# A graph-attention and expert layer on one core: edge loop in written order, node stage in 69 steps

## The chip, the cores and the metric

One NeuronCore of a Trainium2 chip runs the whole program. The metric is the device time of one execution in microseconds (us). The kernel before takes 4170.29 us, the median of 14 runs (4151.29 to 4191.23).

Engines are named as in the profile: PE is the matrix engine (PEld its weight loads), DVE the vector engine, ACT the activation engine, POOL the engine that also writes the descriptors of indirect DMAs, SP the engine that issues most other DMAs. Each engine takes its instructions in one fixed order and waits at the head of its queue.

## The reference, cut to what matters

There are 6250 nodes of 256 features and 206250 edges, sorted by destination. The layer is a transformer convolution over the edges (8 heads of 32), a feed-forward block (FFN) with a gelu, and a mixture of a shared MLP and the best two of four experts.

```python
x0 = layernorm(x)
q, xr, k, v = x0 @ Wq.T + bq, x0 @ Wskip.T + bskip, x0 @ Wk.T + bk, x0 @ Wv.T + bv
e = edge_attr @ We.T                                # 206250 x 256, in heads 8 x 32
alpha = sum(q[dst] * (k[src] + e), axis=-1) / sqrt(32)
w = softmax(alpha over the edges of each dst)
out = segment_sum((v[src] + e) * w, dst)
beta = sigmoid([out, xr, out - xr] @ Wbeta.T)
y = ln1(x0 + beta * xr + (1 - beta) * out)
h = x + ln2(y + gelu(y @ W1.T + b1) @ W2.T + b2)    # gelu by erf, 1024 inner columns
z = layernorm(h)
gates = softmax(z @ gW + gb); top two, softmaxed again
return h + shared_mlp(z) + sum(top two experts(z) * weight)
```

## The kernel before

A first stage (lines 100 to 304) builds tables from the edge list and projects the nodes; it writes `kv_d` (k and v of each node, 2 KB a row), `q_d` and `rn_d` to DRAM. Then `sorted_edges` runs. It has two parts in one Python loop.

**The edge loop.** The edges are 403 blocks of 512, four tiles of 128 each. One pass of the loop works on several blocks at once, as a pipeline over passes:

- `load(i)`, L689 and L691: POOL gathers the k and v rows of block i into the buffer `X` with four indirect DMAs of 128 rows, SP loads the edge features beside them. Pool `fx` has five buffers, and block i+4 is loaded in pass i, so the load of a block waits until `gather` of the block five before it has read its buffer.
- `group(g)`, L645 to L683: for each four blocks, the q rows they need (`qq`, L648) are gathered, stored and loaded again in another layout (`qs`, `qw`), the indicator `oh` (L671) and the folded weights `ws` (L678, L681) are made. The function is a generator; the loop takes one step of it in a pass.
- `score(i+1)`: PE spreads q over the edges (`qg`, L705), DVE multiplies with k (`prod`, L711) and sums over each head (L713).
- `turn(i)`: four PE transposes (L721), an ACT copy to `xT` (L723). `rows(i)`: PE makes the scores (L733), DVE takes their maximum (L737). `weigh(i)`: ACT exponentials with a row sum (L744). `turn_back(i)`: two PE transposes (L752), an ACT copy to `pT` (L754). `gather(i)`: eight PE products (L767, sixteen records in the trace) add up v and edge features by destination. `keep(i)`: DVE picks each head's columns (L775, L778), ACT copies the rest (L777), SP stores the partial sums to `part_d` (L779).

**The node stage.** When all edges of two 125-node blocks are done (`follow`), a generator `ffn` for that pair joins the list `nodes`; there are 25 pairs. `advance(1)`, called three times in a pass, runs the first generator of the list to its next `yield`. Its first part is `merge`: four indirect DMAs (L788) fetch the partial sums of a block into `A`, which has one buffer; DVE weights and adds them (L795 to L821); PE and ACT apply the edge weights (L825 to L833). Then come the gate beta (L405 to L420), the first layer norm (L390 to L429), the FFN (L436 to L463), the second and third norm, the gates, and the shared and expert layers (L484 to L576).

In the FFN one step holds all eight inner column groups: for each, two PE products (L448, four records) and one ACT gelu of 128x250 (L450). After them ACT loads the table set of exponentials again (L451). All PSUM results of the node stage and of `group` share one pool, `f_g`, of three banks.

The order in which the code issues instructions is not the order in which the engines get them: a scheduler orders the whole loop by its own priorities and its own estimate of times, and only what `keep_in_program_order` names stays in place.

Of the kernel before, what the change touches and what calls it, by code (L numbers as in the profile page):

```python
# [40 lines left out]
def gnn_moe_layer(ctx: ExitStack, tc: tile.TileContext, a: dict, out: bass.AP):  # L41
# [322 lines left out]
    def ffn(b0, p3, bank, attention):  # L364
# [67 lines left out]
        def transposed(v, name):  # L432
            tp = bank([128, 2, M])
            for j in range(n):
                for k in range(2):
                    nc.tensor.transpose(tp[:, k, j * NB : (j + 1) * NB],  # L436
                                        v[:, j, k * 128 : (k + 1) * 128], ident[:NB, :NB])
            vT = p3.tile([128, 2, M], F32, name=name, tag="yT")
            nc.scalar.copy(vT, tp)
            return vT  # L440

        yT = transposed(y, "yT")
        yield
        h1 = p3.tile([128, FF // 128, M], F32, name="h1", tag="h1")
        for f in range(FF // 128):
            ps = bank([128, M])
            for k in range(2):
                nc.tensor.matmul(ps, w1[:, k, f * 128 : (f + 1) * 128], yT[:, k, :],  # L448
                                 start=(k == 0), stop=(k == 1))
            nc.scalar.activation(h1[:, f, :], ps, AF.Gelu, bias=b1c[:, f : f + 1])  # L450
        tc.keep_in_program_order(nc.scalar.preload_act_table_set("natural_log_exp_and_others"))  # L451
# [4 lines left out]
        for j in range(n):  # L456
            ps = bank([NB, D])
            for f in range(FF // 128):
                nc.tensor.matmul(ps, h1[:, f, j * NB : (j + 1) * NB], w2[:, f, :],  # L459
                                 start=(f == 0), stop=(f == FF // 128 - 1))  # L460
                if f == FF // 256 - 1:
                    yield
            nc.vector.tensor_tensor(y2[:, j, :], ps, y[:, j, :], ALU.add)  # L463
            yield
# [12 lines left out]
        zT = transposed(z, "zT")  # L477
# [3 lines left out]
        lg = bank([NB, n, NE])  # L481
        for j in range(n):
            for k in range(2):
                nc.tensor.matmul(lg[:, j, :], zT[:, k, j * NB : (j + 1) * NB], gw[:, k, :],  # L484
                                 start=(k == 0), stop=(k == 1))

# [26 lines left out]
        yield  # L513
# [9 lines left out]
        yield  # L523
# [12 lines left out]
        yield  # L536
# [17 lines left out]
        yield  # L554
        wp = bank([128, NE // 2, M])
        for j in range(n):
            for g in range(NE // 2):
                nc.tensor.transpose(wp[:, g, j * NB : (j + 1) * NB], wx[:, j, 2 * g : 2 * g + 2].rearrange("p e d -> p (e d)"),
                                    ident[:NB, :NB])
        nc.vector.tensor_tensor(e2, e2, wp, ALU.mult)  # L560
        wt = bank([NE + 1, M])
        for j in range(n):
            nc.tensor.transpose(wt[:, j * NB : (j + 1) * NB], w[:, j, :], ident[:NB, :NB])
        wT = p3.tile([NE + 1, M], F32, name="wT", tag="wT")
        nc.scalar.copy(wT, wt)
        yield
        for j in range(n):
            cs = slice(j * NB, (j + 1) * NB)
            ps = bank([NB, D])
            nc.tensor.matmul(ps, s2[:, cs], s3w, start=True, stop=False)  # L570
            for g in range(NE // 2):
                nc.tensor.matmul(ps, e2[:, g, cs], e3w[:, g, :], start=False, stop=False)  # L572
            nc.tensor.matmul(ps, wT[:, cs], e3b, start=False, stop=True)  # L573
            nc.vector.tensor_tensor(x2[:, j, :], ps, x2[:, j, :], ALU.add)
        yield
        nc.sync.dma_start(rows_of(out), x2)  # L576

    def sorted_edges(ctx):
# [50 lines left out]
        with tc.tile_pool(name="fd", bufs=3, space=bass.MemoryType.DRAM) as fd, tc.tile_pool(name="fg", bufs=2) as fg, \  # L629
                tc.tile_pool(name="fg1", bufs=1) as fg1, \  # L630
                tc.tile_pool(name="fx", bufs=5) as fx, tc.tile_pool(name="fw", bufs=2) as fw, \
# [5 lines left out]
                tc.tile_pool(name="f_g", bufs=3, space=PSUM) as f_g:  # L637
            groups = {}
            state = {}

            def bank(shape):
                return f_g.tile(shape, F32, name="gp", tag="gp")

            def group(g):
# [4 lines left out]
                                             in_offset=bass.IndirectOffsetOnAxis(ap=idq[:, g : g + 1], axis=0))  # L649
                yield  # L650
# [14 lines left out]
                yield  # L665
                qw = fg.tile([64, GQ * 2, D], BF16, name="qw")
                for u in range(T // 2):
                    nc.sync.dma_start(qw[32 * u : 32 * u + 3 * W],
                                      qs[64 * u : 64 * (u + 1)].rearrange("(m j) (s d) -> (j s) m d", j=W, s=3))
                oh = fg.tile([64, GQ * 2, 128], BF16, name="oh")  # L670
                nc.vector.tensor_scalar(oh[:, : 2 * n], rb[:, : 2 * n], j3[:64], None, op0=ALU.is_equal)  # L671
                yield
# [22 lines left out]
            def score(i):  # L695
# [4 lines left out]
                prod = fw.tile([128, T, D], F32, name="prod")  # L700
# [15 lines left out]
            def turn(i):  # L716
# [5 lines left out]
                xT = fw.tile([K, T, 128], F32, name="xT")  # L722
# [17 lines left out]
            def weigh(i):  # L740
                X3, os, sp = state[i]
                P = fw.tile([128, T // 2, 128], F32, name="P")
# [28 lines left out]
            def keep(i):  # L771

                os, op = state.pop(i)
                ov = fw.tile([128, T // 2, 4, C], F32, name="ov")
                nc.vector.tensor_tensor(ov, op[:, :, : 4 * C].rearrange("p u (h c) -> p u h c", c=C),  # L775
                                        hmc.rearrange("p (o h) c -> p o h c", o=1).to_broadcast([128, T // 2, 4, C]), ALU.mult)
                nc.scalar.copy(os[:, :, C : C + ED], op[:, :, 4 * C :])  # L777
                nc.vector.tensor_reduce(os[:, :, 0:C], ov.rearrange("p u h c -> p u c h"), AX.X, ALU.add)  # L778
# [3 lines left out]
            def merge(b0, n, at):  # L782

                for j in range(n):
                    A = fm.tile([NB, 2, H * PR], F32, name="A", tag="A")
                    for s in range(2):
                        for i in range(2):
                            nc.gpsimd.indirect_dma_start(  # L788
                                out=A[:, s, i * (H // 2 * PR) : (i + 1) * (H // 2 * PR)], out_offset=None,
                                in_=part_d[: 2 * W * tiles_to(b0 + j)], in_offset=bass.IndirectOffsetOnAxis(ap=idp[:NB, b0 + j, s, i : i + 1], axis=0))  # L790
                        yield
                    for _ in range(4):
                        yield
# [18 lines left out]
                    ov = fm.tile([NB, 2, H, C], F32, name="ov", tag="ov2")  # L812
                    oa = fm.tile([NB, 2, H, ED], F32, name="oa", tag="oa")
                    for s in range(2):
                        for v, c0, m in ((ov, 0, C), (oa, C, ED)):
                            nc.vector.tensor_tensor(v[:, s], A4[:, s, :, c0 : c0 + m],  # L816
                                                    w[:, s].rearrange("p (h o) -> p h o", o=1)
                                                    .to_broadcast([NB, H, m]), ALU.mult)
                        yield
                    nc.vector.tensor_tensor(oa[:, 0], oa[:, 0], oa[:, 1], ALU.add)  # L820
                    nc.vector.tensor_tensor(ov[:, 0], ov[:, 0], ov[:, 1], ALU.add)  # L821
                    yield
                    tp = bank([128, H // 2, NB])
                    for i in range(H // 2):
                        nc.tensor.transpose(tp[:, i, :], oa[:, 0, 2 * i : 2 * i + 2].rearrange("p h d -> p (h d)"),  # L825
                                            ident[:NB, :NB])
                    oT = fm.tile([128, H // 2, NB], F32, name="oT", tag="oT")
                    nc.scalar.copy(oT, tp)
                    yield
                    ps = bank([NB, D])  # L830
                    for i in range(H // 2):
                        nc.tensor.matmul(ps[:, i * 2 * C : (i + 1) * 2 * C], oT[:, i, :], web[:, i, :], start=True, stop=True)  # L832
                    nc.vector.tensor_tensor(at[:, j].rearrange("p (h c) -> p h c", c=C), ps.rearrange("p (h c) -> p h c", c=C),  # L833
                                            ov[:, 0], ALU.add)
# [5 lines left out]
            def follow(i):  # L840

                for b0 in range(0, NBLK, 2):
                    b = min(b0 + 1, NBLK - 1)
                    if (tiles_to(b) - 1) // T == i:
                        nodes.append(ffn(b0, p3, bank, merge))
# [7 lines left out]


            AHEAD = 4
            prep = []
            for i in range(-1 - GQ, B + 2):
                if i % GQ == GQ - 2 and 0 <= (i + GQ + 2) // GQ < NG or i == -1 - GQ:
                    prep.append(group(0 if i < -GQ else (i + GQ + 2) // GQ))
                if 0 <= i - 2 < B:  # L860
                    keep(i - 2)
                    follow(i - 2)
                if 0 <= i - 1 < B:
                    weigh(i - 1)
                if 0 <= i + 1 < B:
                    score(i + 1)
                if 0 <= i < B:
                    turn(i)
                if 0 <= i - 1 < B:
                    turn_back(i - 1)  # L870
                advance(1)
# [3 lines left out]
                if 0 <= i - 1 < B:  # L875
                    gather(i - 1)
                if 0 <= i + AHEAD < B:
                    load(i + AHEAD)
                for g in prep[:1]:
                    if next(g, prep) is prep:  # L880
                        prep.pop(0)
# [3 lines left out]
    def any_edges(ctx):  # L885
# [207 lines left out]
        with tc.tile_pool(name="p3", bufs=2) as p3, tc.tile_pool(name="p3_ps", bufs=3, space=PSUM) as p3_ps:  # L1093
            def bank(shape):
                return p3_ps.tile(shape, F32, name="gp", tag="gp")

            for b0 in range(0, NBLK, 2):
                for _ in ffn(b0, p3, bank, fetch):
# [62 lines left out]
```

## Time and profile before

| what | us |
|---|---|
| median of 14 runs | 4170.29 |
| the profiled execution | 4151.98 |
| its span, first to last instruction | 4150.1 |
| before the first L767 | 593.8 |
| from the first to the last L767, 403 passes | 3422.4 |
| after the last L767 | 133.9 |

The three last rows are cut at the starts of the first and the last L767 record. The loop takes 3422.4 / 403 = 8.49 us a pass, or 3422.4 / 25 = 136.9 us for each pair of node blocks. Busy times of the whole span: PE 3039.2 us (73%), DVE 2408.0 (58%), POOL 1979.0 (48%), ACT 1448.7 (35%). The busy time of PE is a model of pipelined instructions, so it says little by itself.

A group row of the profile reads: line, engine, operation, tile written <- tiles read, shapes, count, then busy time and the mean of one in ns, then the idle time just before and what ended it. A row of a windows view has, after the stretch and its length, the busy time of PE, PEld, DVE, ACT and POOL with the number of instructions in brackets, the granted clock of PE as a share, the share of time the 16 DMA engines were busy, and GB/s.

### The profile page before, as it was taken

What the parts mean: (1) busy time and instruction counts of PE and PEld (TensorE: products, weight loads), DVE (VectorE), ACT (ScalarE), POOL (GpSimd) and SP (SyncE); (2) the same over time, 40 slices, a digit from 0 to 9 for tenths busy, and PEclk for the clock granted to TensorE, in tenths of its full rate; (3) what the DMA queues carried; (4) which work ended last, traced back from release to release, by engine and by line L of the source; (5) the groups of instructions that cost most, each with busy time, mean ns of one, the idle gap of its engine ahead of it and who ended that gap; (6) DMA issues with size and microseconds to landing.
All of it is one profiled execution on the core that took longest, in us unless ns stands there. A gap on an engine that the chain in (4) does not pass through costs nothing. (4 is left out here: it accounts for less than half of the span.)

```text
span 4150.1 us, 59098 instructions
## 1 busy us (share of the span) xinstructions
PE 3039.2 (73%) x19362; PEld 1916.7 (46%) x19363; DVE 2408.0 (58%) x5624; ACT 1448.7 (35%) x4313; POOL 1979.0 (48%) x2030
## 2 busy tenths in 40 slices
PE   2566637777778778777877787788778777877876
PEld 1222224454455445544554554455445454544555
DVE  9223235666556656666666566656556665666663
ACT  0111113344333334333433343334334433443332
POOL 0111136654645565555555555555555555555530
PEclk9877856576677677667777776677667767766777
DMA  0333368866766676767767776766676677667730
GB/s 20 113 113 124 123 195 237 217 188 183 205 174 173 189 211 185 195 188 206 192 189 202 201 191 187 203 185 178 179 200 187 181 202 207 181 190 209 200 98 10
DMA packets 611830, 727.33 MB, mean 175 GB/s; under 512 B 384196, under 2 KB 461309, under 8 KB 611514
## 3 DMA queue, kind: packets, MB, share of 16 engines
q0 software_dynamic: 169040, 495.21, 42.6%
q1 hardware_dynamic: 425153, 196.53, 17.9%
q10 hardware_dynamic: 17321, 31.70, 2.1%
q8 instruction: 158, 2.59, 0.3%
q14 instruction: 158, 1.29, 0.1%
HBM read 614.28 MB, written 108.73 MB: 174 GB/s over the span
## 5 line engine op out<-in xcount | busy, mean ns | idle before, releaser
L689 POOL DMA_INDIRECT X<-kv_d,srcT x1612 | 1562.0, 969 | 1257.5 <-issue 380.3
L711 DVE TENSOR_TENSOR prod<-qg,X 128x512 f32<-128x512 f32 x806 | 539.6, 681 | 62.2 <-PE qg L705 38.1
L767 PE MATMUL o<-X,pT 128*32 128x192 f32 x6448 | 502.6, 442 | 17.5 <-ACT pT L754 13.8
L713 DVE TENSOR_REDUCE X<-prod 128x32 f32<-128x1024 f32 x403 | 486.6, 1207 | 0.5
L733 PE MATMUL m<-xT,ws 80*64 80x128 f32 x3224 | 372.8, 367 | 141.4 <-issue 107.9
L705 PE MATMUL qg<-qw,oh 24*128 24x256 bf16 x1612 | 300.3, 341 | 229.1 <-DVE prod L711 132.1
L744 ACT ACTIVATE P<-m,os 128x128 f32<-128x128 f32 x806 | 289.0, 363 | 427.1 <-issue 335.8
L721 PE MATMUL m<-ident,X 128*80 128x128 f32 x1612 | 359.1, 362 | 84.9 <-issue 58.6
L723 ACT COPY xT<-m 80x512 f32<-80x512 f32 x403 | 234.2, 581 | 478.1 <-PE m L721 185.8
L733 PEld LDWEIGHTS m<-xT,ws 80*64 80x64 f32 x3224 | 237.0, 180 | 352.3 <-issue 259.1
L775 DVE TENSOR_TENSOR ov<-o,hmc 128x256 f32<-128x256 f32 x403 | 169.2, 420 | 393.0 <-PE m L752 159.9
L788 POOL DMA_INDIRECT A<-part_d,idp x200 | 249.2, 1246 | 211.8 <-DVE oa L816 89.6
L752 PE MATMUL m<-ident,P 128*128 128x128 f32 x806 | 227.4, 366 | 153.3 <-ACT P L744 76.0
L721 PEld LDWEIGHTS m<-ident,X 128*80 128x80 f32 x1612 | 213.0, 154 | 210.6 <-issue 144.3
L767 PEld LDWEIGHTS o<-X,pT 128*32 128x32 f32 x6448 | 210.3, 136 | 196.3 <-issue 98.6
L737 DVE TENSOR_REDUCE os<-m 128x2 f32<-128x256 f32 x403 | 168.5, 418 | 228.0 <-issue 137.2
L448 PE MATMUL gp<-yT,w 128*128 128x250 f32 x800 | 233.6, 452 | 24.6 <-ACT h L450 12.0
L705 PEld LDWEIGHTS <-oh 24*128 24x128 bf16 x1612 | 77.7, 98 | 351.9 <-issue 341.3
L752 PEld LDWEIGHTS m<-ident,P 128*128 128x128 f32 x806 | 132.0, 184 | 227.9 <-ACT P L744 120.7
L778 DVE TENSOR_REDUCE os<-ov 128x64 f32<-128x256 f32 x403 | 236.0, 586 | 0.1
L448 PEld LDWEIGHTS gp<-yT,w 128*128 128x128 f32 x800 | 179.7, 233 | 68.2 <-issue 16.4
L299 POOL TENSOR_TENSOR qr<-qt 125x256 f32<-125x256 f32 x50 | 33.4, 669 | 359.9 <-ACT qt L297 340.9
(235 smaller groups left out, 4661.0 us busy)
## 6 DMA issues: line engine op xcount, KB each, us to landing
X<-in_edge_dram SPq DMA_DIRECT2D x403, 128.0 KB
part_d<-os SPq DMA_DIRECT2D x403, 98.0 KB
X<-kv_d,srcT POOLq DMA_INDIRECT x1612
qs<-qq SPq DMA_DIRECT2D x101, 192.0 KB
qw<-qs SPq DMA_DIRECT2D x202, 96.0 KB
q_d<-qt ACTq DMA_DIRECT2D x50, 312.5 KB
rb<-rel_d SPq DMA_DIRECT2D x200, 64.0 KB
rn_d<-rn SPq DMA_DIRECT2D x50, 250.0 KB
```

Of the source, the lines that this page charges most:

```text
L448: nc.tensor.matmul(ps, w1[:, k, f * 128 : (f + 1) * 128], yT[:, k, :], start=(k == 0), stop=(k == 1))
L689: nc.gpsimd.indirect_dma_start(out=X3[:, t, : 2 * D], out_offset=None, in_=kv_d, in_offset=bass.IndirectOffsetOnAxis(ap=srcT[:, i, t : t + ...
L705: nc.tensor.matmul(qgs[u][:, c, :], oh[rows, 2 * q + c, :], qw[rows, 2 * q + c, :], start=True, stop=True)
L711: nc.vector.tensor_tensor(prod[:, 2 * u : 2 * u + 2, :].rearrange("p t (s c) -> p t s c", s=2), qgs[u].rearrange("p t (s c) -> p t s c", s ...
L713: nc.vector.tensor_reduce(X3[:, :, 2 * D + ED : 2 * D + ED + H], prod.rearrange("p t (h c) -> p t h c", c=C), AX.X, ALU.add)
L721: nc.tensor.transpose(xp[:K, t, :], X3[:, t, 2 * D :], ident)
L733: nc.tensor.matmul(sp[(t % 2) * 64 : (t % 2 + 1) * 64, t // 2, :], ws[:, t // 2 * 2 * GQ + 2 * q + t % 2].rearrange("k g w h -> k (g w h)" ...
L744: nc.scalar.activation(P[:, u, :], sp[:, u, :], AF.Exp, bias=os[:, u, PR - 1 : PR], accum_out=os[:, u, PR - 2 : PR - 1])
L752: nc.tensor.transpose(pp[:, u, :], P[:, u, :], ident)
L767: nc.tensor.matmul(op[32 * r : 32 * (r + 1), u, :].rearrange("p (s c) -> p s c", s=3), pT[:, u, 32 * r : 32 * (r + 1)], va, start=True, st ...
L778: nc.vector.tensor_reduce(os[:, :, 0:C], ov.rearrange("p u h c -> p u c h"), AX.X, ALU.add)
L788: nc.gpsimd.indirect_dma_start(out=A[:, s, i * (H // 2 * PR) : (i + 1) * (H // 2 * PR)], out_offset=None, in_=part_d[: 2 * W * tiles_to(b0 ...
```

## The change

- The whole edge loop stands in `tc.manual_schedule()`: every engine gets its instructions in the order in which the code issues them.
- The node stage is cut into more steps, 69 for a pair, and `advance(1)` is called five times in a pass. The eight inner column groups are eight steps; each ends with ACT adding the bias (`Identity`) instead of the gelu. One gelu over all 2000 columns follows, then the table load.
- PSUM: `f_g` has two banks, and a new pool `f_h` of one bank (`held`) takes the results that live over several steps. Most of these now have a `yield` between the PE work and the instruction that reads it.
- `fetch` is a stage of its own: A has two buffers, one for each block of a pair, and is fetched four passes after the pair's last block, two indirect DMAs in each of four passes. `ffn` starts ten passes after it. `merge` multiplies in place in `A`.
- `fx` has six buffers and block i+5 is loaded in pass i. `prod`, `xT`, `P` and `ov` have one buffer instead of two.
- `weigh(i)` moves from the start of pass i+1 to the end of pass i. `keep` is split; its ACT copy and store are in `store`, after `turn_back`. `group` starts one pass earlier and has empty steps between its DMAs and their use.

```diff
-            nc.scalar.activation(h1[:, f, :], ps, AF.Gelu, bias=b1c[:, f : f + 1])
-        tc.keep_in_program_order(nc.scalar.preload_act_table_set("natural_log_exp_and_others"))
+            nc.scalar.activation(h1[:, f, :], ps, AF.Identity, bias=b1c[:, f : f + 1])
+            yield
+        nc.scalar.activation(h1, h1, AF.Gelu)
+        ins = nc.scalar.preload_act_table_set("natural_log_exp_and_others")
+        if pin:
+            tc.keep_in_program_order(ins)
...
-            ps = bank([NB, D])
+            ps = held([NB, D])
             for f in range(FF // 128):
                 nc.tensor.matmul(ps, h1[:, f, j * NB : (j + 1) * NB], w2[:, f, :],
                                  start=(f == 0), stop=(f == FF // 128 - 1))
-                if f == FF // 256 - 1:
+                if f % 2 == 1:
                     yield
...
-                tc.tile_pool(name="fx", bufs=5) as fx, tc.tile_pool(name="fw", bufs=2) as fw, \
+                tc.tile_pool(name="fx", bufs=6) as fx, tc.tile_pool(name="fw", bufs=2) as fw, \
...
-                tc.tile_pool(name="f_g", bufs=3, space=PSUM) as f_g:
+                tc.tile_pool(name="f_g", bufs=2, space=PSUM) as f_g, \
+                tc.tile_pool(name="f_h", bufs=1, space=PSUM) as f_h, tc.manual_schedule():
+            AHEAD = 5
...
-            def merge(b0, n, at):
-
-                for j in range(n):
-                    A = fm.tile([NB, 2, H * PR], F32, name="A", tag="A")
+            def fetch(b0):
+
+                rows_of[b0] = []
+                for b in range(b0, min(b0 + 2, NBLK)):
+                    A = fm.tile([NB, 2, H * PR], F32, name="A", tag=f"A{b - b0}")
+                    rows_of[b0].append(A)
                     for s in range(2):
                         for i in range(2):
                             nc.gpsimd.indirect_dma_start(
...
                         yield
...
-                        for v, c0, m in ((ov, 0, C), (oa, C, ED)):
-                            nc.vector.tensor_tensor(v[:, s], A4[:, s, :, c0 : c0 + m],
-                                                    w[:, s].rearrange("p (h o) -> p h o", o=1)
-                                                    .to_broadcast([NB, H, m]), ALU.mult)
+                        nc.vector.tensor_tensor(A4[:, s, :, : C + ED], A4[:, s, :, : C + ED],
+                                                w[:, s].rearrange("p (h o) -> p h o", o=1)
+                                                .to_broadcast([NB, H, C + ED]), ALU.mult)
                         yield
```

The new loop, whole:

```python
prep = []
fetched = []
for i in range(-1 - 2 * GQ, B + 10):
    g, r = divmod(i + 2 * GQ - 1, GQ)
    if r == 0 and 0 < g < NG or i == -1 - 2 * GQ:
        prep.append(group(max(g, 0)))
    if 0 <= i - 2 < B:
        keep(i - 2)
    if 0 <= i + 1 < B:
        score(i + 1)
    advance(1)
    each(prep)
    if 0 <= i < B:
        turn(i)
    if 0 <= i - 1 < B:
        turn_back(i - 1)
    if 0 <= i - 2 < B:
        store(i - 2)
    advance(1)
    if 0 <= i < B:
        rows(i)
    advance(1)
    if 0 <= i - 1 < B:
        gather(i - 1)
    if 0 <= i < B:
        weigh(i)
    advance(1)
    if 0 <= i + AHEAD < B:
        load(i + AHEAD)
    fetched += [fetch(b0) for b0 in after(i - 4)]
    each(fetched)
    nodes += [ffn(b0, p3, bank, held, merge, pin=False) for b0 in after(i - 10)]
    advance(1)
advance(1000)
```

`each` takes one step of every generator in its list; `after(i)` names the pairs whose last edge block is i.

## The prediction

> **What bounds the kernel now.** I read the page first, then the loop cut into stretches, then POOL's waits, then the timeline of one slow pass.
>
> ```profile
> core 0: us, PE busy (x) PEld busy (x) DVE busy (x) ACT busy (x) POOL busy (x), PEclk, DMA share, GB/s
> 593.80:4016.20 3422.40, 2667.42 (x18382) 1719.25 (x18380) 2126.05 (x4857) 1336.06 (x4026) 1875.24 (x1882) 0.71 0.70 192
> 1694.40:1700.40 6.00, 4.83 (x39) 2.38 (x37) 3.24 (x10) 1.90 (x8) 3.44 (x5) 0.50 0.98 256
> 1423.60:1447.40 23.80, 22.57 (x110) 16.35 (x108) 15.99 (x37) 14.62 (x27) 3.78 (x4) 0.82 0.36 103
> ```
>
> Row one is the edge loop. No engine is full: DVE 62%, POOL 55%, ACT 39%, the DMA engines 70%, PE at 0.71 of its clock. Row two is one pass (gather to gather) without node work: 6.00 us, DMA engines 98% busy. Row three is one pass with a whole FFN: 23.80 us, DMA engines 36%, only four gathers. So the loop alternates between passes that the loads pace and passes in which they stand still.
>
> ```profile
> L689 POOL DMA_INDIRECT X<-kv_d,srcT x1612 | 1562.0, 969 | 1257.5 <-issue 380.3 <-PE o L767 365.8 <-PE m L752 115.0
> POOL X L689 <- PE o L767: 365.8, 78, 21.0
> POOL A L788 <- DVE oa L816: 89.6, 8, 24.1
> L450 ACT ACT_TABLE_LOAD x67 | 86.0, 1283 | 1.2
> L744 ACT ACT_TABLE_LOAD x23 | 29.5, 1283 | 0.4
> ```
>
> A load waits for `gather` to free its buffer, once for 21.0 us, or stands behind an A fetch that waits for DVE, up to 24.1 us. The quick pace follows from row one: a gather starts every 1.25 us (0.95 and 0.30 between), four make 5.0, about 1.0 passes until the next buffer is free: 6.0. Of 402 passes 121 take 6.0 to 6.5 us, 97 take 10 or more. The slow ones look like this:
>
> ```profile
> 1427.36 5.22 PE L448 MATMUL gp<-yT,w 128*128 128x250 f32 x12 [0.45 <-issue]
> 1428.27 1.28 ACT L450 ACT_TABLE_LOAD   x1
> 1433.26 1.28 ACT L744 ACT_TABLE_LOAD   x1
> 1435.03 1.28 ACT L450 ACT_TABLE_LOAD   x1
> 1439.62 1.28 ACT L803 ACT_TABLE_LOAD   x1
> 1441.15 1.28 ACT L450 ACT_TABLE_LOAD   x1
> ```
>
> All eight column groups come at once, the scheduler puts edge exponentials between the gelus, and each change of function loads a table; three banks hold PE back until ACT has read them.
>
> **The change, part by part.** I sum over one pair: 16.12 passes (403/25), 136.9 us now. One pass of edge work is 4.17 us on DVE (keep 0.42+0.59, score 0.18+2x0.68+1.21, maximum 0.42); on PE 4.92 at the low clock (qg 0.60, turn 1.06, turn back 0.63, scores 1.12, gather 1.51 in the timeline at 0.50) and 2.96 at full clock (0.40, 0.60, 0.44, 0.66, 0.86); 2.41 on ACT. The 69 steps fall in fixed places: step 1 is the last of a pass, so 2 to 6 fill the next, 7 to 11 the one after. In a pass the first slot lies behind DVE's keep and score and ahead of ACT's `xT`.
>
> Light passes: 2.1 without node steps, and five with little on any engine (steps 7-11, 37-41 with PE warm, 57-61, 62-66, 67-69). POOL paces them at 6.0; I take 6.2. 7.1 x 6.2 = 44.0.
>
> Passes that DVE fills, at 4.3 with `oh` (0.49 in every fourth pass): steps 2-6 add 0.72 of small ones, two products in place, and sums of 1.10. A product of 768 columns has no row: two separate ones are 0.68+0.42=1.10 above, 0.68+0.27 by the slope from 256 to 512 columns; I take 0.95. That gives 8.0; steps 12-16 7.3, 17-21 (0.42, 1.37, 1.36, 1.95) 9.4, 42-46 (0.42, 1.17, 2.22) 8.1. Sum 32.8.
>
> Passes that the written order makes long. Steps 22-24: DVE does keep and score (3.75), the norm's statistics (1.85), ACT the logarithm and exponential (0.6 with handing over), DVE the normalising (2.23), then PE transposes (1.1), and only then may gather (1.5) start: 11.0. Behind these waits queue `xT` on ACT, the maximum on DVE, and with gather the next load. Steps 47-49 likewise: 3.75+1.17+0.6+0.83+1.1+1.5=8.9. Steps 52-56: `xT` comes after a softmax exponential and a relu, at 5.6; scores, gather and three expert steps follow at full clock (0.66+0.86+3x0.9): 9.8. Sum 29.7.
>
> FFN passes. Five column groups on PE: at the low clock eight L448 records took 3.48 us, so 4.92+5x1.74=13.6; at full clock L459 took 6.92 for 32, so 2.96+5x0.84=7.2. The clock came up about 5 us after a dense stretch began (2543 to 2548), so 9.0. The pass with the gelu: load 1.28, gelu, load 1.28, ahead of the edge exponentials. The gelu of 2000 columns has no row: eight of 0.469 are 3.75, one fixed part and the slope of the ACT copies (0.575-0.373 over 244 columns) 1.9; I take 2.0, nearer to one long instruction than to eight. PE waits some 3.3 for it, half covered by scores and gather: 8.5. Sum 17.5.
>
> `group` adds to some passes: PE 0.7+1.45, ACT 0.37 and 2x0.63, one more gather on POOL of 1.25; visible maybe 0.5 four times: 2.0. Its DMAs, the stores and the A fetch (eight of 1.50 in four passes, behind the loads on POOL) I cost at nothing here: POOL needs 16.12x5.0+5.0+12.0=97.6 of the period, and loads run five blocks ahead, so POOL may lag some passes. Without that cover the four passes cost 3 us each. The sixth buffer brings nothing by itself: DVE's `prod` waited 0.3 us for X in all. The table loads fall from 135 to 50, already in these sums; so is SP, whose queue waits for nothing new but `qw` behind an empty step.
>
> 44.0+32.8+29.7+17.5+2.0=126.0 a pair, 3150 for 25: 272 less than 3422.4. The front stays at 593.8, give or take 15 for one more pass of loads. The tail was 133.9; the last two pairs again run alone, each some 58.7 (4084.62 to 4143.28 in the chain of waits) plus 3 for the late gelu, and 7 to the end: 130. Span 593.8+3150+130=3874, with 1.9 around it 3876. The profiled execution was 18 us under the median, so 3894; I say 3900.
>
> On the clock: it stood at 0.50 in the pass without node work and at 0.82 in the pass with the dense FFN. The Trainium skill ("TensorE: Matmul & The Clock Gate", Part 1: The HAM clock gate) says the clock is low by default and released by about 3.4 us of sustained activity. That speaks against cutting the FFN into pieces with edge work between; by the rule taken strictly the dense passes would stay low, and the sum would be that of rival two.
>
> **Rivals.** One, slower: handing over from PE. At 2503.38 PE's transposes ended, yet DVE, ACT, POOL and SP all went on at 2504.1, a microsecond after POOL's last gather; ACT's `xT` waited 185.8 us in 89 such waits, 2.1 each. In written order ACT and DVE stand at a node step's result with edge work behind. If half of a pair's 13.8 node passes pay 2.1 more, the pair takes 140.5 and the kernel 4260; it decides from 5.2 passes (10.9/2.1). For it: the scheduler had kept such waits apart. Against: most `held` results have an empty step first. 13%.
>
> Two, slower: the clock stays at 0.50 in the dense passes. 27-31 then take 13.6, 32-36 12.0, 37-41 11.9, 52-56 13.6, 57-61 10.6: 22 more, 148 a pair, 4445. Half of that is no change. For it: row two. Against: PE would be busy without a gap, and passes after the FFN kept a clock of 1.0 with edge work alone. 8%.
>
> Three, faster: DVE's and PE's excess in one pass is caught up in the next, and POOL alone paces: 16.12x6.05+5.0+12.0=114.5, so 2863 and 3607. For it: before, passes with 7.6 us of DVE work took 6.5 now and then. Against: only one pass lies between score and keep. 26%.
>
> That the change does nothing, because the order moves no work: excluded by the waits of up to 24 us, which come from order alone.
>
> **How the numbers follow.** The forecast has 53%, its own range 3760 to 4030 (the bounds of gelu and product 0.15x100+1.8x25, half to twice the FFN excess, 0.3 a pass either way). Rivals three, one and two have 26, 13 and 8%. The range reaches to rival three and one: 3560 to 4240. Faster by over 0.2%, about what a measurement tells: the forecast but 2% and rival three, 77%; slower 21%; same 2%.
>
> **What would show it.** Right: no pass over 14 us, few under 6; 50 table loads; the DMA share near 0.76 throughout; the longest passes those of steps 22-24 and of the gelu; POOL waiting for L785 often but never for 20 us. Wrong: ACT's L741 or L762 waiting for node products in sum over 400 us (rival one), a loop clock under 0.6 (rival two), a median pass at 6.1 with node steps in it (rival three). A loop in which DVE waits for X would mean the loads fell behind, which I priced at nothing.

## The result, and the profile after it

The changed kernel is slower: 4383.43 us (median of 10 runs) against 4169.87 (47 runs), ratio 1.0512 with a 95% interval of 1.0492 to 1.0532. The forecast was 3900 and faster. The span of the profiled execution is 4382.3 us, where the forecast had 3874. It splits at the first and the last `keep` on DVE (597.27 and 4212.42 us): front 597 (forecast 594), loop 3615 (forecast 3150), tail 170 (forecast 130). So 465 of the 508 us that the forecast lacks are in the loop: 144.6 us for each of the 25 pairs of edge work (3615.15/25) against 126.0, and against 136.9 before.

First the loop as one stretch (busy time of each engine, granted clock, DMA share and rate), then the waits, summed over the span (us, times, longest), and the gelu's line (duration of shortest, median and longest in ns).

```profile
core 0: us, PE busy (x) PEld busy (x) DVE busy (x) ACT busy (x) POOL busy (x), PEclk, DMA share, GB/s
597.27:4212.42 3615.15, 2633.91 (x18372) 1720.28 (x18368) 2234.23 (x4749) 1284.54 (x3962) 1866.07 (x1878) 0.69 0.65 182
```

```profile
POOL X L707 <- PE o L785: 685.3, 152, 10.9
PE m L751 <- ACT xT L741: 478.4, 133, 9.7
DVE os L755 <- PE m L751: 360.1, 166, 4.6
ACT ln_rs L394 <- DVE ln_mv L392: 354.8, 53, 11.0
```

```profile
L453 ACT ACTIVATE h<-h x25: 1869/1870/1871, 902.7 to 4332.2; 128x2000 f32<-128x2000 f32 x25
```

The DMA share fell from 0.70 to 0.65 and no engine is busier than 73%, so nothing became a bound by its work. POOL no longer stands 21 us at a time, but 152 times and 685 us in all: the stops were spread, not removed. PE waits 478 us for `xT`, which edge work needs and ACT makes; ACT in turn stands 355 us at a norm's logarithm. One such pass in the timeline (start and duration in us, in brackets the engine's idle time and what ended it):

```profile
1754.30 0.42 DVE L793 TENSOR_TENSOR ov<-o,hmc 128x256 f32<-128x256 f32 x1
1758.52 0.75 DVE L390 BATCH_NORM_STATS2 ln_st<-t 125x6 f32<-125x256 f32 x2
1759.52 0.30 ACT L394 ACTIVATE ln_rs<-ln_mv,eps 125x2 f32<-125x2 f32 x1 [7.05 <-DVE ln_mv L392]
1759.96 0.56 ACT L741 COPY xT<-m 80x512 f32<-80x512 f32 x1
1760.58 1.12 PE L751 MATMUL m<-xT,ws 80*64 80x128 f32 x8 [8.12 <-ACT xT L741]
1762.34 1.09 PE L436 MATMUL gh<-ident,y 125*128 125x125 f32 x4 [0.64 <-DVE y L429]
1763.36 1.51 PE L785 MATMUL o<-X,pT 128*32 128x192 f32 x16
1765.17 0.95 POOL L707 DMA_INDIRECT X<-kv_d,srcT  x1 [9.63 <-PE o L785]
```

DVE runs `keep`, `score` and the norm's statistics without a gap from 1754.30. ACT stands at L394 for 7.05 us while PE made the input of `xT` (L739) by 1752.0; then everything behind it follows in a row: scores on PE, the transposes L436, only then the gather, and the next load 9.63 us late.

The loop repeats in 16 passes. The table gives each pass by the steps in it, from one `keep` on DVE to the next, median over the 23 pairs whose node steps all lie in the loop, beside the forecast's price and four experiments told of below (e5: no waits between engines in the node stage; e7: no fetch; e8: neither; e13: three repairs). All of them ran on chips of the slower kind.

| steps | forecast | changed | e5 | e7 | e8 | e13 |
|---|---|---|---|---|---|---|
| 2-6 | 8.0 | 7.5 | 7.5 | 7.5 | 7.5 | 7.5 |
| 7-11 | 6.2 | 8.3 | 6.0 | 8.3 | 6.2 | 8.1 |
| 12-16 | 7.3 | 6.9 | 6.9 | 6.9 | 6.9 | 6.9 |
| 17-21 | 9.4 | 11.9 | 11.5 | 11.9 | 10.4 | 11.9 |
| 22-26 | 11.0 | 10.6 | 7.6 | 10.6 | 7.6 | 10.6 |
| 27-31 | 9.0 | 8.1 | 6.3 | 7.7 | 7.3 | 8.1 |
| 32-36 | 8.5 | 8.4 | 8.3 | 8.3 | 8.9 | 8.3 |
| 37-41 | 6.2 | 10.9 | 6.6 | 9.9 | 6.6 | 8.7 |
| 42-46 | 8.1 | 10.6 | 9.7 | 10.6 | 9.8 | 10.4 |
| 47-51 | 8.9 | 9.3 | 5.4 | 9.3 | 5.5 | 8.2 |
| 52-56 | 9.8 | 10.8 | 13.7 | 10.5 | 7.9 | 10.9 |
| 57-61 | 6.2 | 9.1 | 9.2 | 6.7 | 6.7 | 9.1 |
| 62-66 | 6.2 | 13.7 | 8.7 | 13.9 | 6.2 | 10.0 |
| 67-69 | 6.2 | 8.1 | 10.3 | 5.9 | 7.6 | 9.1 |
| none, or 1 | 6.2 | 6.1 | 6.0 | 6.1 | 6.1 | 6.0 |

The five passes priced as light (7-11, 37-41, 57-61, 62-66, 67-69) take 50.1 us instead of 31.0. That is 19.1 of the 23.2 us by which a pair's 14 passes with node steps miss their prices (134.2 against 111.0, to which the 2.0 of `group` come). The longest pass, 62-66, was among the ones priced lowest:

```profile
1829.92 1.21 POOL L811 DMA_INDIRECT A<-part_d,idp  x1 [0.30 <-issue]
1832.00 0.42 DVE L755 TENSOR_REDUCE os<-m 128x2 f32<-128x256 f32 x1 [3.47 <-PE gh L564]
1834.72 1.22 DVE L731 TENSOR_REDUCE X<-prod 128x32 f32<-128x1024 f32 x1
1835.86 0.67 DVE L567 TENSOR_TENSOR e<-e,gh 128x500 f32<-128x500 f32 x1
1836.67 0.57 PE L570 MATMUL gh<-ident,w 125*5 125x125 f32 x2 [4.32 <-DVE X L731]
1837.04 1.06 PE L739 MATMUL m<-ident,X 128*80 128x128 f32 x4
1838.19 0.58 ACT L741 COPY xT<-m 80x512 f32<-80x512 f32 x1 [4.51 <-PE m L739]
1842.16 1.51 PE L785 MATMUL o<-X,pT 128*32 128x192 f32 x16
```

PE wants to write the gate weights' transposes (L570) into the one `held` bank, which DVE frees with L567, and DVE has all of `keep` and `score` ahead of that. PE stands 4.32 us (the row names L731, but L567 ends at 1836.53, just ahead of L570), and the edge's own transposes L739 stand behind L570. DVE's 3.47 us at L755, ahead of the pass, are another wait: PE had made these scores by 1828.6, and DVE went on 0.87 us after POOL's gather of A ended. More of this below.

### The profile page after: what moved, and what is told of

It is laid out like the page before. It is cut to its first block, busy times and chain, and to the rows that moved or that the text cites. A ratio compares the mean times of both kernels' runs of the same rounds, so it can differ in the third digit from the quotient of the medians.

```text
span 4382.3 us, 58358 instructions
## 1 busy us (share of the span) xinstructions
PE 3018.7 (69%) x19362; PEld 1922.7 (44%) x19363; DVE 2522.0 (58%) x5524; ACT 1399.2 (32%) x4254; POOL 1972.8 (45%) x2030
## 3 DMA queue, kind: packets, MB, share of 16 engines
q1 hardware_dynamic: 425153, 196.53, 16.5%
## 4 chain that ended last, share of the span: by engine, by line
PE 42%; DVE 19%; issue 10%; ACT 5%; DMA 2%; POOL 1%; another core or an unknown queue 1%; DVEq 0%; SPq 0%; ACTq 0%; POOLq 0%
PE gh L464 6%; PE gp L449 5%; PE o L785 5%; PE m L751 4%; PE m L739 4%; PE gp L511 3%; DVE prod L729 3%; DVE X L731 3%; PE qg L723 2%; PE m L770 2%; PE gh L582 2%; PE gp L696 1%; PE gh L859 1%; DVE A L840 1%; PE gh L436 1%
## 5 line engine op out<-in xcount | busy, mean ns | idle before, releaser
L751 PE MATMUL m<-xT,ws 80*64 80x128 f32 x3224 | 350.9, 354 | 609.6 <-ACT xT L741 478.4
L729 DVE TENSOR_TENSOR prod<-qg,X 128x512 f32<-128x512 f32 x806 | 518.0, 684 | 264.0 <-PE qg L723 189.2
L751 PEld LDWEIGHTS m<-xT,ws 80*64 80x64 f32 x3224 | 223.9, 173 | 746.9 <-ACT xT L741 539.5
L755 DVE TENSOR_REDUCE os<-m 128x2 f32<-128x256 f32 x403 | 170.5, 423 | 631.5 <-PE m L751 360.1
L731 DVE TENSOR_REDUCE X<-prod 128x32 f32<-128x1024 f32 x403 | 491.7, 1220 | 13.9
L785 PE MATMUL o<-X,pT 128*32 128x192 f32 x6448 | 465.1, 421 | 0.6 <-ACT os L799 0.6
L741 ACT COPY xT<-m 80x512 f32<-80x512 f32 x403 | 233.7, 580 | 486.2 <-issue 227.5
L739 PE MATMUL m<-ident,X 128*80 128x128 f32 x1612 | 339.0, 349 | 19.3 <-issue 17.4
L464 PE MATMUL gh<-w,h 128*125 128x256 f32 x800 | 262.4, 474 | 71.4 <-ACT h L453 62.2
L785 PEld LDWEIGHTS o<-X,pT 128*32 128x32 f32 x6448 | 201.4, 132 | 177.6 <-issue 104.0
L739 PEld LDWEIGHTS m<-ident,X 128*80 128x80 f32 x1612 | 226.2, 151 | 89.3 <-issue 43.1
L449 PE MATMUL gp<-yT,w 128*128 128x250 f32 x800 | 249.6, 449 | 1.4 <-ACT yT L440 1.3
L795 DVE TENSOR_REDUCE os<-ov 128x64 f32<-128x256 f32 x403 | 239.0, 593 | 13.8
L464 PEld LDWEIGHTS gh<-w,h 128*125 128x125 f32 x800 | 173.5, 233 | 131.1 <-ACT h L453 70.9
L770 PE MATMUL m<-ident,P 128*128 128x128 f32 x806 | 207.3, 349 | 21.3 <-issue 13.0
L723 PE MATMUL qg<-qw,oh 24*128 24x256 bf16 x1612 | 206.6, 342 | 9.6 <-issue 7.1
L449 PEld LDWEIGHTS gp<-yT,w 128*128 128x128 f32 x800 | 164.8, 225 | 58.5 <-issue 32.8
```

Source lines behind the costliest of these rows:

```text
L723: nc.tensor.matmul(qgs[u][:, c, :], oh[rows, 2 * q + c, :], qw[rows, 2 * q + c, :], start=True, stop=True)
L729: nc.vector.tensor_tensor(prod[:, 2 * u : 2 * u + 2, :].rearrange("p t (s c) -> p t s c", s=2), qgs[u].rearrange("p t (s c) -> p t s c", s ...
L731: nc.vector.tensor_reduce(X3[:, :, 2 * D + ED : 2 * D + ED + H], prod.rearrange("p t (h c) -> p t h c", c=C), AX.X, ALU.add)
L739: nc.tensor.transpose(xp[:K, t, :], X3[:, t, 2 * D :], ident)
L751: nc.tensor.matmul(sp[(t % 2) * 64 : (t % 2 + 1) * 64, t // 2, :], ws[:, t // 2 * 2 * GQ + 2 * q + t % 2].rearrange("k g w h -> k (g w h)" ...
L770: nc.tensor.transpose(pp[:, u, :], P[:, u, :], ident)
```

## The experiments

Theory A: in written order a node step that waits for another engine stands at the head of its queue, with edge work behind it. The batches of experiments ran on different chips: the kernel before took 4145 to 4182 us on three of them, and 3844 on two (e1 to e4; e14 and e15). Ratios are to the kernel before on the same chip.

**Order, place and fetch.** e1 drops the written order (and, as in the kernel before, pins the table load behind the gelu):

```diff
-                tc.tile_pool(name="f_h", bufs=1, space=PSUM) as f_h, tc.manual_schedule():
+                tc.tile_pool(name="f_h", bufs=1, space=PSUM) as f_h:
```

> Only the written order is taken back: the scheduler orders the same instructions (one gelu, products in place, fetch ahead, six buffers). Theory A, the written order puts edge instructions behind node steps that wait (the five passes called light take 50.1 us a pair, not 31.0): most of the 18.6 us a pair of excess goes, 3900 to 4100. Rival B, the rest of the change (gelu of 2000 columns, merge in place, fetch on POOL) is what costs: 4300 or more.

Measured 3653 us, ratio 0.951 (0.945 to 0.956). Being on a faster chip, it was run again in a later batch:

> The scheduler's order with all the rest of the change, beside the other kernels of this batch. If the order alone is what makes the changed kernel slow, its ratio stays near 0.95 on this chip too, and under the 0.977 of the same kernel with eight gelus; if it was the faster chip that favoured it, 0.98 to 1.00.

0.976 (0.970 to 0.982), between the two cases: part of the 0.951 seems to have been the faster chip. The order alone separates 0.976 from 1.052: rival B falls, and all other parts of the change together are a gain.

e2 writes the five `advance(1)` of a pass behind its edge work, as one `advance(5)` behind the load.

> All five node steps of a pass are written behind the edge work and the load. Theory A: ACT's xT no longer waits for a norm (7.05 us once a pair) and PE's gather no longer for the last expert products; the pair falls by 10 to 20 us, 3900 to 4150. Rival C, handovers of PE held while POOL gathers, or the low clock, set the pass whatever the place of the steps: 4300 or more.

4328 us, ratio 1.126 (1.118 to 1.134) on the faster chip, where rival C had it. A miss for theory A as I put it. The passes of e2 hold steps 1-5, 6-10 and so on: the one of 61-65 takes 7.1, but 36-40 takes 15.4, 1-5 12.4 and 66-69 13.8. In 36-40 PE stands 3.74 us for the gelu with the next block's `qg` behind it, since the two now follow each other directly. So the distance of a step from the one that feeds it seems to decide as well as its place; no run here tries the distance alone.

e3 starts the fetch at `after(i - 8)` in place of `after(i - 4)`.

> The eight A gathers of a pair move four passes later, out of steps 57 to 66 into the passes with few steps. Rival C, the hold: the pass of steps 62 to 66 falls from 13.7 to about 9 and that of 57 to 61 from 9.1 to 7.5, 6 us a pair, 4230. Theory A: the products and handovers of these steps stay in front of the gather, at most 3 us a pair, 4310 to 4380.

4482 us, ratio 1.165 (1.158 to 1.171), outside both forecasts. It came too late for the merge (DVE waited 431.8 us for A), one pass a pair took 20.2. Still it answered: without A gathers in it, 57-61 fell to 6.8, while 62-66 stayed at 14.1, so the fetch isn't what makes that one long.

e4 leaves out the node stage and its fetch.

> The node stage and its fetch are left out; the edge loop and its groups stay in written order. If edge work alone keeps POOL's pace, 6.0 to 6.3 us a pass, some 3050 in all; if the written order of edge work itself costs, 7 or more a pass, 3400.

2745 us in a single run, 5.3 us a pass: less than expected, on the faster chip. A stretch of it (columns as in the first windows view):

```profile
700.00:2700.00 2000.00, 1520.45 (x13692) 919.19 (x13688) 1489.73 (x2724) 829.81 (x2910) 1511.83 (x1595) 0.71 0.96 282
```

Here the DMA engines, 96% busy, set the pace, at 282 GB/s; in the light pass of the first chip, 98% busy, they moved 256. So no wait of the written order shows in edge work alone.

> The changed kernel once more, on the chip of this batch, since the kernel before took 3844 us on the chip of the last four runs and 4170 on the first. If written order and not the transfers sets its pace, it stays at 4340 to 4390 also where the kernel before is faster, and its ratio to it is 1.13 to 1.14; if transfers set it, it keeps its ratio of 1.05.

4351 us, ratio 1.052 (1.048 to 1.056), but the chip was one of the slower, so the question of the ratio on a faster one stayed open.

> The kernel before with a profile on the chip of this batch: where it is faster than 4170 its light passes, which took 6.0 us at 256 GB/s, should be the part that shrank, to 5.3 or so.

4142 us, a single run: a slower chip, nothing new.

**The waits themselves.** e5 keeps every node instruction but takes its operand from a constant tile where another engine makes it, for instance

```diff
-            nc.scalar.copy(vT, tp)
+            nc.scalar.copy(vT, Z(128, 2, M))
...
-                nc.tensor.matmul(ps, h1[:, f, j * NB : (j + 1) * NB], w2[:, f, :],
+                nc.tensor.matmul(ps, Z(128, NB), w2[:, f, :],
```

> The changed kernel with every node instruction in its place, on its engine and in its size, but each operand that another engine makes is read from a constant tile: the node stage's values are not the reference's, and no node step waits for another engine. Theory A, steps that wait for another engine stand at the head of a queue: the five passes called light fall from 50 to 35 us a pair or less and the whole to 3500 to 3800. Rival D, the amount of node work in a pass, its place or the clock: at most 5 us a pair less, 4230 or more.

3904 us, ratio 0.942 (0.938 to 0.945). The same instructions, of the same length (DVE's in the loop add up to 2425 and 2426 us), and 453 us less than after_again by the two profiles: 359 in the loop (14.4 a pair), 91 in the tail (73 in place of 164). Against after_again, on the same chip, the passes 7-11, 22-26, 37-41, 47-51 and 62-66 fell by 2.2, 3.0, 3.7, 3.9 and 5.0. The whole is above what theory A expected, and far from rival D. The light sum fell to 40.8 only, because 57-61 and 67-69 stayed long and 52-56 grew to 13.7. There the A gathers fall:

```profile
1972.94 0.60 PE L756 MATMUL m<-ident,X 128*80 128x128 f32 x4
1973.88 1.20 POOL L828 DMA_INDIRECT A<-part_d,idp  x1 [0.30 <-issue]
1975.38 1.21 POOL L828 DMA_INDIRECT A<-part_d,idp  x1 [0.30 <-issue]
1977.74 1.22 ACT L716 COPY ws<-gp 64x512 f32<-64x512 f32 x2 [5.32 <-remote]
1978.98 0.58 ACT L758 COPY xT<-m 80x512 f32<-80x512 f32 x1
1979.61 1.12 PE L768 MATMUL m<-xT,ws 80*64 80x128 f32 x8 [3.61 <-ACT xT L758]
```

PE had done L756, and the matmuls that L716 reads before it, by 1973.6; ACT went on at 1977.74, 1.15 us after POOL's last gather ended, and the semaphore by which PE reports to ACT moved at 1977.72. I call this a held report; it is rival one of the prediction. e7 takes the gathers of A away (those of the loads stay):

```diff
+                if b0:
+                    rows_of[b0] = rows_of[0]
+                    return
```

> The changed kernel without the fetches after the first pair's: later pairs merge the first pair's rows again, so their outputs are not the reference's; all else stays. Passes 52 to 69, into which the eight A gathers of a pair fall, take 41.6 us now. If PE's reports are held until POOL's gathers end (the rival of the prediction), they fall by 10 to 15 us a pair, ratio to the kernel before 0.96 to 0.99. If only steps that wait for each other make them long, at most 4 us a pair, ratio 1.02 to 1.05.

Ratio 1.013 (1.007 to 1.019): between the two. The chip is another than that of after_again; by the profiles it is 4.6 us a pair (137.9 against 142.5), all of it in 52 to 69, and by the ratios about 6.5. The pass 62-66 kept 13.9. With e5's edit as well:

> Both taken away: no fetch after the first pair's, and every operand of a node step that another engine makes read from a constant tile (values not the reference's). If waits between node steps and the hold behind A gathers are two causes, their gains add: 14 us a pair from the one (measured with the fetch in place) and 10 to 15 from the other, ratio 0.85 to 0.88. If the one only uncovers the other, ratio 0.91 to 0.94, as without handovers alone.

0.866 (0.861 to 0.870), 116.8 us a pair. So these are two causes, and each hides part of the other: the waits between steps are worth 14.4 with the fetch and 21.1 without it (each on one chip), the fetch 4.6 with the waits and 11.3 without (each between two chips). e9 yields after each A gather, not after two:

> The eight A gathers of a pair one a pass over eight passes, from one pass earlier, in place of two a pass over four. If the length of POOL's unbroken run of gathers sets the hold, runs of five instead of six shorten the long passes but touch twice as many: 0 to 8 us a pair less, ratio 1.00 to 1.05. If each node step's own wait sets the pass, no change, 1.045 to 1.06.

1.055 (1.049 to 1.061), no change: 57-61 fell to 7.8 and 67-69 to 7.2, but 7-11 rose to 9.7 and the passes without steps from 6.1 to 7.4.

**Parts.** e6 is e1 with eight gelus in place of eight copies and one gelu.

> The scheduler's order as in e1, but eight gelus of 250 columns in place of eight copies and one gelu. If the single gelu and its fewer table loads are what makes e1 faster than the kernel before, this one is within 1% of the kernel before; if fetching ahead and the products in place are, it stays within 1% of e1, 4 to 5% under the kernel before.

0.977 (0.974 to 0.979), the same as e1_again on another of the slower chips, with 192 table loads against 54. Where the scheduler orders, one gelu or eight makes no difference that these intervals (0.6% either way) can show, though 138 loads of 1.283 us are 177 us of ACT. So neither the loads nor the single gelu make e1 faster than the kernel before; which of the other parts does was not tried.

e10, e11 and e12 repair one wait each in the written order, e13 all three.

```diff
-        wt = held([NE + 1, M])
+        wt = bank([NE + 1, M])
```

> The transposed gate weights go into one of the two rotating banks, not the single held one, so PE no longer stands ahead of the edge's turn until DVE has read that bank behind keep and score. Theory A: the pass of steps 62 to 66 falls from 13.7 to 8 to 10 us, the others stay, ratio 1.01 to 1.03. If POOL's gathers hold that pass, it stays above 12 and the ratio at 1.045 or more.

1.037 (1.032 to 1.042). The pass named, 62-66, fell from 13.7 to 10.0, just within what was said; but the one behind it rose by 1.1, so the gain is 1.5%, not 2 to 4.

```diff
                     store(i - 2)
+                flush()
```

with the norm's two activations put on a list that `flush` empties.

> The norms' logarithm and exponential are written behind the pass's two transposes' copies and the store's copy on ACT, not ahead of them; no step changes its slot. Theory A: ACT no longer stands 7 us at the norm with xT behind it; passes of steps 22 to 26 and 47 to 51 fall by 1.5 to 3 us each (from 10.6 and 9.3), ratio 1.01 to 1.035. Rival E, DVE's own work and its waits fill these passes: under 0.5 us each, ratio 1.04 or more.

1.039 (1.034 to 1.044), close to rival E's side. The pass 47-51 fell by 1.1; 22-26 did not move. The waits of e11 tell where it went:

```profile
PE gh L449 <- DVE y L442: 218.2, 25, 10.0
PE gh L449 <- DVE y L413: 163.9, 25, 6.8
PE m L764 <- ACT xT L754: 117.8, 139, 8.5
```

PE's wait for `xT` fell from 481 us to 118, and 382 now stand at the transposes of the normed rows (50 times), ahead of the gather.

```diff
-        nc.scalar.activation(h1, h1, AF.Gelu)
+        for f in range(0, FF // 128, 2):
+            nc.scalar.activation(h1[:, f : f + 2, :], h1[:, f : f + 2, :], AF.Gelu)
```

> The gelu of 2000 columns as four of 500, in the same place between the same two table loads. Theory A: PE's second FFN layer starts on the first quarter, the pass of steps 37 to 41 falls from 10.2 to 8.5 to 9.5 us, ratio 1.035 to 1.048. If the gelu's and the loads' time on ACT with edge work behind is what counts, the pass grows by 0.5, ratio 1.05 to 1.06.

1.031 (1.025 to 1.037): the pass 37-41 fell to 7.3, more than expected. The second layer of the FFN in the changed kernel, then in e12:

```profile
1781.22 1.87 ACT L453 ACTIVATE h<-h 128x2000 f32<-128x2000 f32 x1
1783.14 3.78 PE L464 MATMUL gh<-w,h 128*125 128x256 f32 x8 [2.62 <-ACT h L453]
1786.86 0.60 PE L723 MATMUL qg<-qw,oh 24*128 24x256 bf16 x4
```

```profile
1612.17 2.15 ACT L454 ACTIVATE h<-h 128x500 f32<-128x500 f32 x4
1612.84 3.59 PE L465 MATMUL gh<-w,h 128*125 128x256 f32 x8 [1.29 <-ACT h L454]
1616.37 0.39 PE L724 MATMUL qg<-qw,oh 24*128 24x256 bf16 x4
```

PE waits 1.29 in place of 2.62, and the `qg` behind runs at full clock (0.39 against 0.60). With the wait PE also loses its clock, as the changed kernel shows in three stretches, ahead of the wait, in it and behind it:

```profile
1778.00:1780.50 2.50, 2.04 (x27) 1.04 (x26) 0.88 (x3) 2.46 (x6) 0.00 (x0) 1.00 0.60 188
1780.50:1783.14 2.64, 0.03 (x4) 0.00 (x0) 2.01 (x5) 2.61 (x3) 2.01 (x2) 0.84 0.58 159
1787.00:1789.00 2.00, 2.00 (x8) 1.32 (x5) 1.47 (x3) 0.00 (x0) 0.00 (x0) 0.50 0.47 162
```

The clock (third figure from the end) was 1.00, fell within the wait, and was still 0.50 four microseconds behind it. It fell to 0.50 in this wait (2.5 to 2.7 us) or within 2 us behind it in all 23 such passes of the changed kernel; in e12 (1.3 to 1.4 us) it did in 9 of 23, for some 3 us, in the pass above until 1616.3. Over the pass 37-41 the mean clock rose from 0.72 to 0.92. The Trainium skill ("TensorE: Matmul & The Clock Gate", Part 1: The HAM clock gate) puts the low clock after at least one idle window of about 3.4 us; here shorter waits were followed by it, so on this kernel the measurement and not that figure decides.

> All three at once. If the three waits are separate, their gains add: the pair falls by 8 to 12 us, ratio 0.97 to 1.00. If one only uncovers the other, no better than the best of the three, 1.01 to 1.03. Under 0.976 it would also beat the scheduler's order.

1.012 (1.007 to 1.017): the gains add up to most of their sum (4.0% of 4.8), less than expected, and the written order still loses to the scheduler's 0.976. e14 moves the third `advance(1)` behind `gather` and `weigh`.

> As e13, and the third node step of a pass behind the gather and the edge exponentials in place of ahead of them. Theory A: the gather of the pass of steps 22 to 26 no longer stands behind the transposes; that pass falls from 10.6 to about 9 us, which DVE's keep, score and norm fill (3.8 and 1.8 and 2.2, with 0.6 for ACT), that of steps 47 to 51 by about 1, ratio 0.985 to 1.005. If DVE's work sets these passes already, no change, 1.008 or more.

4043 us, ratio 1.052 (1.047 to 1.056) on a chip where the kernel before takes 3844, so the expected ratios don't apply. The passes do: 22-26 fell from 10.6 to 8.4 and 47-51 from 8.2 to 6.1 (e3 had 10.6 and 9.3 on such a chip). Other passes grew against e13, 37-41 from 8.7 to 9.9 and 52-56 from 10.9 to 12.5, and PE waits elsewhere, 188 us for `group`'s gather; so what the move is worth in all is not shown.

> The scheduler's order with the gelu in four pieces and the gate weights' transposes in a rotating bank. If the single bank and the single gelu cost only where the order is written, no change from the scheduler's 0.976 on this kind of chip (0.965 to 0.985; 0.95 on the faster chip). If they are costs of the work itself, 0.94 to 0.96 here.

3540 us, ratio 0.921 (0.914 to 0.929), against 0.951 for e1 on a chip with the same time of before. So the two repairs mend something under the scheduler too, which I hadn't expected; which of them was not tried. It is the fastest version, faster than both kernels.

## Why the prediction was wrong

- **Light passes, 7.1 x 6.2 = 44.0.** The step that failed. Their work was summed nearly rightly: without waits and fetch (e8) the five with node steps take 33.3, against 31.0. They take 50.1 because their steps wait for another engine: 37-41 for the gelu (e12), 62-66 for a bank (e10), 7-11 for DVE's sums (PE waits 3.9 us for them ahead of each, and in e5 the pass takes 6.0); 57-61 and 67-69 are long because of the A fetch (6.7 and 5.9 in e7). I had called them light on every engine, and a handover from one engine to another is not work on any.
- **DVE-filled passes, 32.8.** 36.9. 2-6 and 12-16 were right, and DVE never stands in them. 17-21 and 42-46 are each 2.5 too low, because DVE does not fill them: it stands 2.9 and 3.0 us, in the one most of it (2.3) at the maximum for PE's scores, in the other there (1.2) and at `prod` for PE's `qg` (1.3). e5 and e8 take 0.4 to 1.5 of each away; what the rest hangs on was not tried.
- **Written-order-long passes, 29.7.** 30.7. Here I had added the waits in a row by hand, and 11.0, 8.9, 9.8 came to 10.6, 9.3, 10.8. The method was right where I used it; I used it on three passes of fourteen. That 52-56 fits is partly luck: without the fetch and the waits it takes 7.9.
- **FFN passes, 17.5.** 16.5. The gelu took 1.87 (2.0 said), a product of 768 columns 0.95 (0.95). But PE's wait for the gelu, booked here as half covered, falls in the next pass, which I had at 6.2.
- **The A fetch at nothing, 12 if its cover is gone.** 4.6 a pair as it stands, 11.3 once the other waits are gone. That POOL may lag was no full cover; held reports, as in e5, are one way in which a late POOL stops the others.
- **25 pairs.** The sum has the node passes of 25 pairs in the loop and of the last two in the tail once more. In the loop there are 23, so by its own prices it was some 48 us too high (2 x 24.2, what the 14 passes cost over 6.2 each), which hid a part of the miss: a pair's node passes are 23.2 off, not 18.6. Of the kernel before, 85 passes take 10 us or more from `keep` to `keep`, not 97.
- **Tail, 130.** 170. More than half of it is waits between steps: 73 in e5, against 164 in after_again.
- **Rival one, 140.5 a pair.** The right sign and the nearest price, given 13%. Its sign was put in the wrong place: ACT waits 355 us at the norm itself (L394), in front of L741, and the 478 us stand one engine on, at PE's L751. Its mechanism, reports of PE held while POOL gathers, is real, but at the one handover counted here it did not grow. Where DVE's maximum stood waiting for PE's scores, it started over 0.5 us after PE's end 99 times in the changed kernel (151 us in all), and 74 times in the kernel before (151 us). The waits for L567, at L394 and for the gelu, shown above, are plain waits for DVE or ACT. The 185.8 us from which the rival took its 2.1 are all of ACT's waits for `xT`'s transposes, held or not. How the 14.4 us of e5 divide between the two kinds is not shown, since the loads' gathers stay in every run.
- **Rivals two and three.** The loop's clock is 0.69 after 0.71, and 27-31 takes 8.1, not 13.6, so two is out as the main cause; the clock lost in a wait shows in e12. Three, POOL's pace, is not what e4 shows for edge work alone (there it is the transfers' pace); in written order with node steps intact no version came to its 114.5 a pair, while e1 took 115.3 and e15 111.3 in the scheduler's order on the faster chips.
- **Other signs.** 50 table loads: right (48 in the loop, 54 in all). Three passes are over 14 us where none was to be, two are under 6, and the longest by the table are 62-66, not those of 22-24 and the gelu. POOL waits for L785 often, at most 10.9 us: right. DMA share 0.65, not 0.76.

Settled: the written order makes it slow (e1_again), by waits between node steps (e5, e10, e12) and, behind those, by the fetch (e7, e8). Open: whether all that the fetch costs is held reports, since nothing took the hold away and left the gathers in place; and how the changed kernel stands on the faster chips.

## What to carry to other kernels

When work of two kinds shares queues in a fixed order, price each pass as a chain: for every instruction that needs another engine's result, ask what that engine has ahead of it and what stands behind the one that waits. A sum of work by engine is the time only if nothing waits: here the five light passes took 33.3 us with waits and fetch away (e8), 31.0 by the sum, and 50.1 as they stand. That e5's 3904 us lie beside the forecast's 3900 is luck: its light passes take 40.8 us, and those of 22-26, 47-51 and 52-56 together 26.7 where the forecast had 29.7. Time the same parts under a scheduler's order before fixing one by hand: here they were 2.4% faster than the kernel before with the scheduler and 5.2% slower in written order.

## What the runs showed of the hardware

- The chips differ: in the experiments' batches the kernel before took 4145 to 4182 us on three, 3844 on two. With the DMA engines all but full the rate was 256 GB/s on the first chip and 282 on one of the faster.
- Results of PE reached ACT late while POOL ran a row of indirect gathers: 4.6 us late in e5, 1.15 us after POOL's last gather ended. In the changed kernel 99 of the 264 waits of DVE's maximum for L751 ended over 0.5 us after PE's end; in e7, without the gathers of A, 109 of 263.
- The clock fell to 0.50 in or just behind a wait of PE of 2.5 to 2.7 us in 23 of 23 cases (changed kernel), of 1.3 to 1.4 us in 9 of 23 (e12).
- 138 more table loads (192 against 54, 1283 ns each) changed no time that can be told where the scheduler ordered the work (0.977 against 0.976, each within 0.6%).
